# Layer 2 of a cross-attention kernel: scores of the first query half ahead of the values of two groups back

## The chip, the cores and the metric

One Trainium2 chip, of which one core is used. A core has five engines that run their own instruction streams and wait for each other through semaphores: TensorE (PE; its weight loads are shown as PEld), VectorE (DVE), ScalarE (ACT), GpSimd (POOL) and SyncE (SP, which here only issues transfers). Matmul results land in PSUM, which has eight banks of 128 x 512 floats; all else lies in SBUF. The metric is the device time of one execution in microseconds; three executions of the kernel before took 1634.38, 1636.12 and 1638.09 us, so the median is 1636.12 us.

## The reference

Two cross-attention layers, one after the other, on `x` of shape (16, 256, 320) with a context of (16, 256, 512): 16 batches, 256 queries, 320 channels in 20 heads of 16, 252 text tokens and 4 image tokens. Each layer does this (cut; `l2norm` only in the second):

```python
text, ip = ctx[:, :-4], ctx[:, -4:]
q, k, v = x @ Wq, text @ Wk, text @ Wv                # in heads of 16
text_out = softmax(q_h @ k_h.T * scale) @ v_h         # 256 x 252 scores per head
scores   = q_h @ k_ip_h.T * scale                     # 256 x 4 per head
# layer 1 adds to the image scores a term from softmax(q @ k.T) over all channels
# layer 2 adds a similarity to the image scores and
# normalises, with l2norm, what it attends to
out = (text_out + mask * softmax(fused) @ v_ip_h) @ Wout + bout + x
```

All of it is in fp32. The kernel keeps that precision by splitting operands into a rounded high part and a remainder, so a product of two fp32 matrices becomes several matmuls.

## The kernel before

The unit of work is a *slot*: one group of four heads of one batch. Layer 1 is slots 0 to 79 (`slot0`), layer 2 slots 80 to 159 (`slot1`, 16 batches x 5 groups); slots 160 and 161 finish. Slot functions are generators: they yield pieces of work, and between them a number, the place in the slot up to which a list of other tasks with due times is run (`fill`): projections of queries (L528), keys and values (L205), the end of a batch (`close1`), the opening of a later one, transfers of rows (`stacks`). These *fill tasks* differ from slot to slot and repeat every five slots.

In a slot of layer 2, for group k:

- `attend1(k - 2)`: P, the values of the group two slots back, 16 matmuls of 128 x 32 weights (L823) into one PSUM bank, then W, 16 more with the remainder `wt` against a constant (L826). `settle1` follows it: DVE transposes the bank into `nt` (L870), takes a reciprocal (L873) and multiplies into `hsn` (L874); POOL copies the norm parts (L871).
- `both1(k, 0)`: T, the transposed scores of group k for the first key half (4 matmuls, L775, two PSUM banks); S, the scores of group k + 2 for the first query half (4 matmuls, L780, a tile of two banks); DVE's reduction of S to row maxima `mn` (L781); and two exponentials on ACT from T into P (L786). `both1(k, 1)` is the same for the second half.
- `norm1(k - 1, u, n)`: products of the rounded weights `ctb` with `gm` (L814), in groups of 4 and 3 matmuls, four groups per slot, called (0,0), (0,1), (1,0), (1,1). DVE multiplies each group's bank into `wt` (L815), which also frees the bank.
- `rounded1`: ACT rounds P into `ctb` (L804), POOL writes the remainder to `wt` (L805).
- `maxima(k + 2)`: two matmuls (L792) turn the maxima, ACT copies them (L794) and issues two transfers into the query rows (L796). T of group k + 2 reads them as an extra row; it makes the exponential of a score less its maximum.

Only PE's order is fixed, by the order of the program; the order on DVE, ACT and POOL and the PSUM bank of each tile are chosen by a scheduler when the program is built (`schedule_with_timeline_sim=True, auto_bufs=True`). Tiles have tags: S (one tile of two banks), T (2), P (1) and X (3), the last for all else. P in SBUF has four buffers, two per slot: the exponentials of group k write the buffers that the values of group k - 2 read.

Two kinds of slots come up below. In the last part of one slot per batch `close1` does three small products (L931) whose results DVE adds to `hT` (L932). In the next slot ACT rounds `hT` (L517) and DVE makes the remainder `ho` (L518, L519), on which L528 runs later. Called here the slot before the split and the slot with the split.

Of the kernel before, what the change touches and what calls it, by code (L numbers as in the profile page):

```python
# [37 lines left out]
NS = B * NG  # L38
# [10 lines left out]
def xattn2(  # L49
# [39 lines left out]
    def bank(tag="X"):  # L89
        return ps.tile([128, 512], F32, tag=tag, name=tag, bufs=BANKS[tag])  # L90

    def scores():

        return ps.tile([128, 1024], F32, tag="S", name="S", bufs=1).rearrange("p (h t) -> p h t", h=4)
# [4 lines left out]
    def buf(tag, shape, dtype=F32, bufs=1, name=None):  # L99
        if tag in ("wB", "wD", "vr", "raw"):  # L100
            return sb.tile(shape, dtype, tag=tag, name=name or tag, bufs=bufs)
        size = 1
        for d in shape[1:]:
            size *= d
        if tag not in slots:
            slots[tag] = [0, dtype] + [const_tile([128, max(size, words.get(tag, 0))], f"{tag}_{i}", dtype) for i in range(bufs)]
        n, kind, *ring = slots[tag]
        assert kind == dtype and len(ring) == bufs, tag
        slots[tag][0] += 1
        t = ring[n % bufs][: shape[0], :size]  # L110
        names = "abcd"[: len(shape) - 1]
        if len(names) > 1:
            t = t.rearrange(f"p ({' '.join(names)}) -> p {' '.join(names)}", **dict(zip(names, shape[1:])))
        return t
# [26 lines left out]
    def anchor(inst):  # L141
        anchors[inst.ins.engine] = inst
        return inst
# [540 lines left out]
    def attend0(k):  # L684
        b, g = divmod(k, NG)
        v, pv = get("v0", b), bank("P")
        for vt in range(3):
            values0(k, pv, v, vt)
        settle0(b, g, pv)
# [68 lines left out]
        yield from project(l, wo[l], hh, evac)  # L758
        return y

    def both1(k, t):

        a = k + 2 < 2 * NS and QK[k + 2] 
        c = NS <= k < 2 * NS and QK[k]
        if a:
            if t == 0:
                maxes[k + 2] = buf("mn", [128, 4, 4], FR, bufs=2)[:, :2]
            sp = scores()
        if c:
            st = [bank("T").rearrange("p (h t) -> p h t", h=2) for u in range(2)]  # L770
            lo = (0, DUP)[t]
            for j in range(2):
                for u in range(2):
                    rows = slice(64 * u, 64 * u + KS1)
                    mm(st[u][:, j], c[1][rows, j, lo : lo + 128], c[0][rows, j], start=True, stop=True)  # L775
        if a:
            for j in range(2):
                for u in range(2):
                    rows = slice(64 * u, 64 * u + XROW)
                    mm(sp[:, 2 * u + j], a[0][rows, j, t * 128 : (t + 1) * 128], a[1][rows, j], start=True, stop=True)  # L780
            anchor(nc.vector.tensor_reduce(maxes[k + 2][:, t], sp[:, :, :T1], axis=AX.X, op=ALU.max))  # L781
        if c:
            for u in range(2):
                if t == 0:
                    P[k, u] = buf("P", [128, 2, 2, S], bufs=SIZES["NP"])
                anchor(nc.scalar.activation(P[k, u][:, t], st[u], AF.Exp, scale=SCALE))  # L786
# [13 lines left out]
    def rounded1(k, u):  # L800
        R[k, u] = buf("ctb", [128, 2, 2, S], FR, bufs=SIZES["CTB"], name="ph")
        W[k, u] = buf("wB", [128, 2, 2, S], bufs=SIZES["WB"], name="wt")
        for t in range(2):
            nc.scalar.activation(R[k, u][:, t], P[k, u][:, t], AF.Copy, scale=0.5)  # L804
            anchor(nc.gpsimd.tensor_sub(W[k, u][:, t], P[k, u][:, t], f(R[k, u][:, t])))  # L805
# [3 lines left out]
    def norm1(k, u, n):  # L809

        gm = get("t1", k // NG - B)[1]
        yp = bank().rearrange("p (h t) -> p h t", h=2)
        for i, (gb, kt) in enumerate(blocks[n]):
            mm(yp, gm[:, gb], R[k, u][:, kt], start=i == 0, stop=i == len(blocks[n]) - 1)  # L814
        nc.vector.tensor_mul(W[k, u][:, n], yp, W[k, u][:, n])  # L815

    def attend1(k):
        b, g = divmod(k - NS, NG)
        v, pv = get("t1", b)[0], bank("P")
        for n in range(2):  # L820
            for s in range(4):
                h = V1W * (4 * g + s)
                mm(pv[32 * s : 32 * s + 32, :S], v[:, n, h : h + 32], P[k, s % 2][:, n, s // 2], start=n == 0, stop=False)  # L823
        for n in range(2):
            for s in range(4):
                mm(pv[32 * s : 32 * s + 32, :S], zone, W[k, s % 2][:, n, s // 2], start=False, stop=n == 1)  # L826
        settle1(b, g, pv)

    def slot1(k):
        last = k - 1 if NS < k <= 2 * NS else None  # L830
        mine = k < 2 * NS
        if k == NS:
            yield lambda: maxima(k + 1)
        elif k == NS + 1:
            yield lambda: attend0(k - 2)
        else:
            yield lambda: attend1(k - 2)
        yield lambda: both1(k, 0)
        if last:
            yield lambda: norm1(last, 0, 0)  # L840
        yield 0.33
        if last:
            yield lambda: norm1(last, 0, 1)
        yield lambda: both1(k, 1)
        if mine:
            yield lambda: rounded1(k, 0)
        yield lambda: stacks(k + LEAD)
        if last:
            yield lambda: norm1(last, 1, 0)
        yield 0.67  # L850
        if last:
            yield lambda: norm1(last, 1, 1)
        if mine:
            yield lambda: rounded1(k, 1)
        yield lambda: maxima(k + 2)
        yield 1.0
# [3 lines left out]
    def settle1(b, g, pv):  # L860
        hn = hsn
        if g == 0:
            norms[b] = buf("tmp", [128, NG, 8, 6], bufs=2, name="n1")
        nt = norms[b]
        if "na" not in w1:
            w1["na"], masks = [buf("nt", [128, 2, 8, 32], bufs=2, name="na") for i in range(2)]
            w1["bmask"] = masks.rearrange("p a f c -> p (a f c)")[:, :CP]
            dma(w1["bmask"], bmask_d)
        na = w1["na"][:, (NG * b + g) % 2]
        nc.vector.transpose(na.rearrange("p f c -> p (f c)"), pv[:, :S])  # L870
        nc.gpsimd.tensor_copy(nt[:, g], na[:, :, 16:22])  # L871
        rz = pv[:, S : S + 8]
        nc.vector.reciprocal(rz, na[:, :, 16])  # L873
        nc.vector.tensor_mul(  # L874
            hn[:, g // 2, :, g % 2], na[:, :, 0:16], rz.unsqueeze(2).to_broadcast([128, 8, 16])
        )
        if g == NG - 1:
            nc.gpsimd.tensor_copy(hn[:, 2, :, 1], hn[:, 2, :, 0])
            later(0.4, lambda: gather(1, b))
# [98 lines left out]
    def get(*key):  # L978
        while key not in results:
            step(key)  # L980
        return results[key]
# [27 lines left out]
    for c in range(B // 2):  # L1009
        n, k = 10 * c, [("k0", c)] if c else []  # L1010
# [30 lines left out]
    def stacks(k):  # L1041
        if 0 <= k < 2 * NS:
            (stacks0 if k < NS else stacks1)(k)

    def ahead(k, t):
        if k < NS:
            score0(k, t)
        else:
            both1(k - 2, t)

    def maxima(k):
        if k < 2 * NS:
            (maxima0 if k < NS else maxima1)(k)
# [41 lines left out]
    with tc.manual_schedule(engines=PINNED):  # L1095
        for k in range(2 * NS + 2):
            clock[0] = k
            for part in (slot0 if k < NS else slot1)(k):
                if callable(part):
                    part()  # L1100
                else:
                    fill(k + part)
        fill(999)
# [81 lines left out]
```

## Time and profile before

| what | value |
|---|---|
| median of three executions | 1636.12 us |
| the profiled execution, its span | 1630.48 us, 1628.7 us |
| granted TensorE clock, mean over the span | 0.974 |
| layer 2, steady part (840 to 1550 us) | granted clock 1.00 |
| PE / DVE / POOL / ACT busy, whole span | 94% / 74% / 73% / 51% |
| matmuls of layer 2, 780 to 1600 us: L814, P, W, T, S | 316.4, 82.4, 81.4, 76.6, 62.0 us busy |
| DVE reduction L781, 128 x 1008 | 160 of 1195 ns |
| ACT exponential L786, 128 x 512 | 320 of 597 ns |
| period of a batch in the steady part (P at 1000.24 and at 1055.44) | 55.20 us |

A row of the timeline gives the start in microseconds, the busy time of the group, engine, line, operation, output and input, tile and count, and in brackets the idle time before it and who ended it. Matmul ends are modelled, and consecutive groups overlap in the table; the time from one start to the next says what a group costs PE.

### The profile page before, as it was taken

The numbers are of one execution on the slowest core, as the hardware profiler recorded it, in microseconds if no ns is written. First come the engines' busy times: TensorE is split into PE (matmuls) and PEld (weight loads), VectorE is DVE, ScalarE is ACT, GpSimd is POOL, SyncE is SP. The second block draws the span as 40 slices with busy tenths as digits, with TensorE's granted clock in tenths as the row PEclk, the third lists the DMA queues.
The fourth block names the chain that finished last, engine by engine and source line by source line (L and its number), as shares of the span: only waits on it lengthen the run. The fifth ranks groups of instructions, "written<-read, shape, count | busy, mean of one in ns | idle before, by whom it ended". The sixth has DMA issues, their size and how long they took to land.

```text
span 1628.7 us, 36230 instructions
## 1 busy us (share of the span) xinstructions
PE 1533.9 (94%) x13306; PEld 1232.8 (76%) x13306; DVE 1209.1 (74%) x2410; ACT 830.2 (51%) x1797; POOL 1189.4 (73%) x1147
## 2 busy tenths in 40 slices
PE   7899999999999898789999999999999999999996
PEld 6677878787878777577777777777777777777765
DVE  5567777777777668778877787778777877778685
ACT  5345455555555545445555555555554555555462
POOL 3358787878787767777678767866877687668676
PEclk9799999999999999899999999999999999999998
DMA  7767677767676666665514342433244334323301
GB/s 218 201 203 203 199 193 219 202 204 206 202 208 198 181 206 172 164 187 171 159 62 129 108 139 84 135 110 125 89 134 120 110 103 127 127 89 102 108 26 45
DMA packets 235741, 243.06 MB, mean 149 GB/s; under 512 B 19050, under 2 KB 219468, under 8 KB 235564
## 3 DMA queue, kind: packets, MB, share of 16 engines
q1 hardware_dynamic: 233356, 239.44, 49.4%
q8 instruction: 106, 1.74, 0.4%
q10 hardware_dynamic: 2208, 1.30, 0.3%
q14 instruction: 71, 0.58, 0.1%
HBM read 116.78 MB, written 88.18 MB: 126 GB/s over the span
## 4 chain that ended last, share of the span: by engine, by line
PE 52%; DVE 15%; POOL 11%; DMA 9%; ACT 6%; issue 4%; SPq 2%; ACTq 0%; POOLq 0%; DVEq 0%
PE X L205 15%; PE X L814 9%; PE X L528 7%; PE P L709 5%; POOL wt L805 4%; PE S L652 3%; POOL P L682 3%; PE P L823 3%; DMA qs<-qd 3%; PE P L826 2%; PE T L676 2%; PE T L775 2%; DVE wt L815 2%; DMA kd<-kst 2%; DVE mn L781 2%
## 5 line engine op out<-in xcount | busy, mean ns | idle before, releaser
L682 POOL TENSOR_TENSOR P<-P,rs 128x512 f32<-128x512 f32 x320 | 413.2, 1312 | 157.4 <-ACT P L679 157.0
L805 POOL TENSOR_TENSOR wt<-P,ctb 128x512 f32<-128x512 f32 x320 | 422.4, 1336 | 120.3 <-ACT ctb L804 118.7
L814 PE MATMUL X<-ctb,gm 128*128 128x512 f32 x1120 | 328.8, 411 | 2.5 <-DVE wt L815 2.5
L679 ACT ACTIVATE P<-T 128x512 f32<-128x512 f32 x320 | 175.9, 595 | 221.4 <-PE T L676 106.1
L786 ACT ACTIVATE P<-T 128x512 f32<-128x512 f32 x320 | 174.2, 597 | 144.1 <-PE T L775 123.3
L815 DVE TENSOR_TENSOR wt<-X,wt 128x512 f32<-128x512 f32 x320 | 216.7, 678 | 24.9 <-PE X L814 22.5
L804 ACT ACTIVATE ctb<-P 128x512 fp32r<-128x512 f32 x320 | 195.7, 631 | 73.1 <-PE X L814 57.9
L814 PEld LDWEIGHTS X<-ctb,gm 128*128 128x128 f32 x1120 | 188.8, 188 | 49.4 <-DVE wt L815 5.2
L781 DVE TENSOR_REDUCE mn<-S 128x4 fp32r<-128x1008 f32 x160 | 191.1, 1195 | 0.8 <-PE S L780 0.8
L654 DVE TENSOR_REDUCE mn<-S 128x4 fp32r<-128x716 f32 x160 | 142.6, 891 | 0.0
L676 PE MATMUL T<-qs,ks 127*128 127x256 f32 x640 | 112.1, 295 | 22.0 <-DMA qs<-mt 10.2
L709 PE MATMUL P<-P,vr 128*32 128x256 f32 x1920 | 129.4, 404 | 2.2 <-DVE mx L581 2.2
L652 PE MATMUL S<-ks,qs 125*128 125x256 f32 x640 | 117.4, 307 | 5.4 <-DVE mn L654 2.0
L652 PEld LDWEIGHTS S<-ks,qs 125*128 125x128 f32 x640 | 88.2, 194 | 41.8 <-issue 34.0
L894 POOL TENSOR_TENSOR r<-u,rs 128x40 f32<-128x40 f32 (+2 forms) x17 | 108.7, 6394 | 14.8 <-DVE u L891 14.7
L528 PE MATMUL X<-ho,wF 128*128 128x256 f32 x768 | 112.8, 290 | 6.4 <-DVE ho L518 3.0
L528 PE MATMUL X<-hq,wE 128*128 128x256 f32 x768 | 110.1, 287 | 7.5 <-ACT hq L517 3.2
L676 PEld LDWEIGHTS T<-qs,ks 127*128 127x128 f32 x640 | 92.8, 198 | 27.0 <-DVE tmp L726 11.6
L528 PEld LDWEIGHTS X<-ho,wF 128*128 128x128 f32 x768 | 103.5, 195 | 12.1 <-DVE ho L518 4.7
L528 PEld LDWEIGHTS X<-hq,wE 128*128 128x128 f32 x768 | 102.4, 193 | 12.0 <-ACT hq L517 3.6
L205 PE MATMUL X<-cta,wA 128*128 128x252 f32 (+1 forms) x720 | 100.6, 286 | 8.7 <-ACT wA L147 6.3
L205 PEld LDWEIGHTS X<-cta,wA 128*128 128x128 f32 x720 | 93.8, 194 | 15.2 <-ACT wA L147 6.5
(197 smaller groups left out, 2807.5 us busy)
## 6 DMA issues: line engine op xcount, KB each, us to landing
qd<-q SPq DMA_DIRECT2D x96, 384.0 KB
qs<-tph SPq DMA_DIRECT2D x64, 308.0 KB
kd<-kst SPq DMA_DIRECT2D x73, 256.0 KB
rawc<-in_cT_dram SPq DMA_DIRECT2D x60, 256.0 KB
qs<-qd SPq DMA_DIRECT2D x80, 192.0 KB
ks<-kd SPq DMA_DIRECT2D x80, 192.0 KB
ks<-kd SPq DMA_DIRECT2D x160, 96.0 KB
qs<-qd SPq DMA_DIRECT2D x160, 96.0 KB
```

Of the source, the lines that this page charges most:

```text
L205: last = mm(out, lhs(a, k), rhs(b, k), start=i == 0, stop=i == len(terms) - 1)
L528: mm(pp, w(s, k, slice(m * 128, (m + 1) * 128)), a[:, t], start=i == 0, stop=i == len(terms) - 1)
L652: mm(sp[:, h], Q[: XROW + T0, h, t * 128 : (t + 1) * 128], K[: XROW + T0, h], start=True, stop=True)
L676: mm(st[p][:, j], K[:KS0, 2 * p + j, t * 128 : (t + 1) * 128], Q[:KS0, 2 * p + j], start=True, stop=True)
L679: exp = anchor(nc.scalar.activation(pt, st[p], AF.Exp, scale=SCALE))
L682: anchor(nc.gpsimd.tensor_mul(pt, pt, rs[:, t : t + 1].to_broadcast([128, 2, S])))
L709: mm(pv[32 * s : 32 * s + 32, o : o + S], v[:, vt, h : h + 32], P[k, s // 2][:, t, s % 2], start=vt < 2, stop=vt != 1,)
L781: anchor(nc.vector.tensor_reduce(maxes[k + 2][:, t], sp[:, :, :T1], axis=AX.X, op=ALU.max))
L804: nc.scalar.activation(R[k, u][:, t], P[k, u][:, t], AF.Copy, scale=0.5)
L805: anchor(nc.gpsimd.tensor_sub(W[k, u][:, t], P[k, u][:, t], f(R[k, u][:, t])))
L814: mm(yp, gm[:, gb], R[k, u][:, kt], start=i == 0, stop=i == len(blocks[n]) - 1)
L815: nc.vector.tensor_mul(W[k, u][:, n], yp, W[k, u][:, n])
```

## The change

The values of two groups back no longer open the slot. They are handed to `both1(k, 0)` as a function, which calls it after the reduction of S and before the exponentials. In slots 82 to 159 PE's order at the slot's opening was P, W, T, S and is now T, S, P, W; `settle1` moves with P and W. In slots 160 and 161, which have no scores, the order stays. Nothing is added or taken away. DVE's, ACT's and POOL's orders and the banks are chosen anew by the scheduler.

```diff
-    def both1(k, t):
+    def both1(k, t, between=None):
 
         a = k + 2 < 2 * NS and QK[k + 2] 
         c = NS <= k < 2 * NS and QK[k]
...
             anchor(nc.vector.tensor_reduce(maxes[k + 2][:, t], sp[:, :, :T1], axis=AX.X, op=ALU.max))
+        if between:
+            between()
         if c:
             for u in range(2):
                 if t == 0:
...
             yield lambda: maxima(k + 1)
         elif k == NS + 1:
             yield lambda: attend0(k - 2)
-        else:
-            yield lambda: attend1(k - 2)
-        yield lambda: both1(k, 0)
+        yield lambda: both1(k, 0, (lambda: attend1(k - 2)) if k > NS + 1 else None)
         if last:
             yield lambda: norm1(last, 0, 0)
         yield 0.33
```

As built, DVE has the reduction of the first S ahead of L870, L873 and L874 in nearly all slots of layer 2; in the slot with the split it stands directly behind L519. ACT issues the L796 transfers behind the exponentials in one slot per batch. SP's order is the same. The banks of layer 2 were shared among all tags; now S has two of its own, T two, P one, and X goes round three.

## The prediction

> **What bounds the kernel now.** I read the page's head and its busy table first, then the table by windows, then the waits of PE, and last the rows of PE and DVE over one batch of layer 2. The whole program:
>
> ```profile
> span 1628.7 us, 36230 instructions
> PE 1533.9 (94%) x13306; PEld 1232.8 (76%) x13306; DVE 1209.1 (74%) x2410; ACT 830.2 (51%) x1797; POOL 1189.4 (73%) x1147
> 1000.00:1050.00 50.00, 49.21 (x440) 38.02 (x439) 37.45 (x71) 26.65 (x56) 37.18 (x37) 1.00 0.34 106
> ```
>
> PE is busy for 94% of the span. The third line is a window of layer 2, the only layer that the change touches: PE 49.21 of 50 us at a granted clock of 1.00, DVE 37.45, ACT 26.65, POOL 37.18. No other engine is near to its end there, so only two things can move the time: PE's own cost of another order, and the little that PE waits. The waits of PE between 780 and 1600 us:
>
> ```profile
> PE S L780 <- DVE mn L781: 7.1, 14, 1.1
> PE X L814 <- DVE wt L815: 2.5, 13, 0.2
> ```
>
> Scores wait for the reduction that empties S, and the norm products wait for a bank, once per batch. These are idle times after modelled ends. Counted from start to start they are larger, as the rows of one batch show (first two slots of five):
>
> ```profile
> 998.04 1.46 PE L931 MATMUL X<-rs,rs 128*128 128x256 f32 x6
> 999.21 0.99 PE L814 MATMUL X<-ctb,gm 128*128 128x512 f32 x3
> 1000.24 1.07 PE L823 MATMUL P<-P,v1t 128*32 128x256 f32 x16
> 1001.13 1.05 PE L826 MATMUL P<-wt,zone 128*32 128x256 f32 x16
> 1002.11 0.50 PE L775 MATMUL T<-qs,ks 50*128 50x256 f32 x4
> 1002.45 0.40 PE L780 MATMUL S<-ks,qs 48*128 48x256 f32 x4
> 1002.78 1.19 PE L814 MATMUL X<-ctb,gm 128*128 128x512 f32 x4
> ...
> 1005.98 0.50 PE L775 MATMUL T<-qs,ks 50*128 50x256 f32 x4
> 1006.97 0.50 PE L780 MATMUL S<-ks,qs 48*128 48x256 f32 x4 [0.49 <-DVE mn L781]
> 1007.66 1.19 PE L814 MATMUL X<-ctb,gm 128*128 128x512 f32 x4 [0.19 <-DVE wt L815]
> ```
>
> Undisturbed, T to S takes 1002.45 - 1002.11 = 0.34 and S to L814 0.33. In the second half of this slot they take 0.99 and 0.69, so 0.65 + 0.36 = 1.01 us are lost. The cause is DVE in the same slot:
>
> ```profile
> 994.77 0.45 DVE L921 STREAM_TRANSPOSE rs<-rs 128x256 f32<-128x256 f32 x1 [1.23 <-POOL rs L914]
> 995.31 1.19 DVE L781 TENSOR_REDUCE mn<-S 128x4 fp32r<-128x1008 f32 x1
> ...
> 1001.64 1.59 DVE L518 TENSOR_TENSOR ho<-hT,ho 128x512 fp32r<-128x512 f32 x1 [0.30 <-ACT ho L517]
> 1003.15 1.51 DVE L519 SCALAR_TENSOR_TENSOR ho<-ho,tmask,hT 128x256 fp32r<-128x256 f32 x1
> ...
> 1005.75 1.16 DVE L781 TENSOR_REDUCE mn<-S 128x4 fp32r<-128x1008 f32 x1
> ```
>
> S was full at 1002.85, but its reduction started at 1005.75, behind the split of ho (3.1 us) and L922, L739 and the L870 transpose. This is the slot with a spell of long DVE work; the three other slots of the batch lose nothing at S. The slot before loses about 0.24 (0.11 at S, 0.13 at L792). Fourteen whole batches of 55.2 us lie in the steady part.
>
> **The change, part by part.** In slots 82 to 159 PE issued P (L823), W (L826), T, S; it now issues T, S, P, W. Slots 160 and 161 hold neither scores nor exponentials and keep their order. No matmul, reduction, copy or transfer is added; SP's queue is unchanged in the built program.
>
> *PE's own cost.* From the rows: P to W 0.89, W to T 0.98, T to S 0.34, S to L814 0.33, together 2.54. Behind the same predecessor, T starts after the same time as P (L792: 0.21 in both cases; L205 with wA: 1.57 in both). W is left in 0.98 for L814 too (the one such place, 1597.17 to 1598.15). So the new order costs 0.34 + (S to P) + 0.89 + 0.98, and only S to P is not in the trace. The nearest row is S to L814, 0.33: with it the sum is 2.54 again, and the cost nothing. Bounds: products to P start 0.13 earlier than products to products (L528: 0.95 against 1.09), and T to S and S to X differ by under 0.1, so at best 0.24, -0.09 per slot; at worst P and its 32-column weights cannot be set up beside S, and the 0.18 by which other entries differ is added, +0.19. Over the 76 slots that have both S and P: -6.8 to +14.4 us. I take 0 by the nearest row.
>
> The Trainium skill speaks against the change here: "TensorEngine Tiling (Array Packing)", Tiling Modes, Key Properties, says that changing the tiling mode drains TensorE, and S (row tiles) to P (column tiles) is such a change. Priced as S's busy 0.40 less the 0.33 after which its successor starts, a drain would give 0.07 x 76 = +5 us. The row speaks for less: S to L814 is a change of mode as well and takes 0.33, and both orders hold three changes per first half.
>
> *The slot before the split of ho (990.84 to 1000.24).* S starts at 990.84 + 0.34 = 991.18 instead of 993.05. Its reduction fits into the 1.23 us in which DVE waits for POOL's L914 (993.3 to 994.8), where nothing covers it now. Then L921 994.77, L870, L873, L874, and wt00 (L815) starts at 996.08 instead of 996.43; everything behind it is 0.35 earlier, wt10 ends at 999.39 instead of 999.74. But in the built program the X tiles of layer 2 go strictly round three banks, where before they also used others. The third product of L931 must have the bank of the L814 group three tiles back, which wt10 frees: it starts at 999.45, where the run of matmuls alone gives 998.66. From there L814 0.33, L792 0.70, next slot 0.21: 1000.69 against 1000.24. So +0.45: the wait at S goes, and a larger one at L931 comes.
>
> *The slot with the split.* T 1000.69, S 1001.03, P 1001.36, W 1002.25, L814 1003.23, and by the durations of the rows T 1006.43, S 1006.77 with no wait, as the reduction now stands directly behind L519. L517 starts 0.19 later (its three L932 follow the late L931), so L518 1001.83, L519 1003.34, reduction 1004.78, L922, L739, L870, then wt00 from 1007.05 to 1007.72. The second L814 group waits for that bank: 1007.78, against 1007.66 now. Thus the 1.01 at S and L814 has gone, but the time was DVE's, whose chain L517 to wt00 is as long as before. The batch ends +0.12, x 14 = +1.7 us.
>
> *The bank ring elsewhere.* In the other slots the reuse comes 0.06 to 0.8 us after the release, by the present rows; cost nothing, but the cover is thin. *ACT:* exps now wait for P of two groups back, whose buffers they overwrite; they start some 0.6 us earlier than now all the same. In one slot per batch the two transfers of the maxima (L796) are issued behind them, about 2 us later; T needs them more than 9 us after the issue. L804 and L147 queue behind the exps as before. *DVE:* settle (L870, L873, L874) comes after the reduction; hsn is read again at L739 more than 5 us later. *POOL:* L871 moves behind one L148 (1.29 us) in one slot per batch; only the image softmax 5 slots on reads it.
>
> *Ends of the layer.* At 782.82 W waits for wt11 (W takes 1.72 to T, not 0.98); it now comes 0.67 later in the slot: -0.7. At 1555.33 T to S takes 1.55 through the same wait as above, in a slot with no L931 in it: -1.2.
>
> Sum: 0 + 1.7 - 0.7 - 1.2 = -0.2 us. The profiled execution took 1630.48 us (span 1628.7), 5.6 less than the median of 1636.12; the difference carries over to the median: 1635.9. A change under 0.2% (3.3 us) cannot be told from none for this kernel.
>
> Apart from the sum: the Trainium skill, "SBUF — State Buffer", Who interferes with whom, says that a DVE instruction with two SBUF inputs and a GpSimd instruction that reads SBUF contend for a port pair, and that the later one blocks fully. L518 at 1.59 us beside POOL's L805, and 0.69 at 1603.95 without it, agree. By that rule L519 ends with POOL's instruction however late it began, and the batch would come out at -0.08 instead of +0.12, -2.8 us in all.
>
> **The rivals.**
> A, *DVE's relief is real* (faster). The third product of L931 does not wait, or waits half. For it: 1.24 us of waits per batch stand at exactly these places, and DVE is idle 1.23 us where the reduction would now go. Against it: wt10 frees the bank. If all goes: -1.24 x 14 - 1.9 = -19 us (1617); with half of it about -9 (1627).
> B, *S to P costs* (slower). Its place is each of 76 slots; from 0.043 us per slot it decides (3.3 / 76). At 0.1, +7.6 (1643.5); at 0.19, +14.4 (1650). Against it: leaving S costs 0.33 wherever else it is left.
> C, *the ring of three banks bites oftener* (slower). The margins of 0.06 to 0.8 us fall short in more slots, or the whole ho chain is shifted by the 0.45 too: +0.4 per batch, +5.6 (1641.5); up to +0.9, 1648.5.
> That the reduction does not move is excluded: in the built DVE order it stands before the transpose.
>
> **How the numbers follow.** Forecast (within about 3 us of 1635.9) 0.40; A 0.29; B 0.14; C 0.17. The forecast alone spans 1632 to 1639.5. The range reaches to three quarters of A and to two thirds of B and C: 1620 to 1645. Faster: A and 0.06 of the forecast, 0.35. Slower: B, C and 0.03 of it, less 0.01 of C that stays inside, 0.33. Same: 0.32.
>
> **What would show it.** In the changed profile: S to P of 0.33; no wait of S for mn in the second halves; waits of about 0.8 at L931 or the L814 behind it, released by DVE wt; L814 after the second S 0.7 after it in the split slot; the batch still 55.2 us long. A batch of 54 us speaks for A; one of 55.7 with S to P near 0.43 for B; one of 55.6 with new waits at L814, L205 or L792 for C. A late T behind L796 would prove the ACT reading wrong.

## The result, and the profile after

In comparisons of fifteen runs each, the changed kernel took 1628.12 us (1624.5 to 1633.45) and the kernel before 1633.88 us (1628.77 to 1638.09). The ratio is 0.9971 with a 95% interval of 0.9961 to 0.9981: 0.29% faster, 3.1 to 6.4 us, about 4.7. The forecast was no change that can be measured (1635.9 us, -0.2 us), the range 1620 to 1645. The time lies in the range, but the interval of the ratio excludes 1: there is a gain, a small one.

The profiled execution of the changed kernel is the longer of the two, 1631.7 against 1628.7 us:

```profile
span 1631.7 us, 36363 instructions
PE 1540.0 (94%) x13306; PEld 1235.5 (76%) x13306; DVE 1215.7 (75%) x2410; ACT 828.8 (51%) x1797; POOL 1188.4 (73%) x1147
```

That is not the change. The first T of layer 2 starts at 750.8 us in this trace and at 744.3 in that of the kernel before, after instructions that are the same in both programs; in the traces of this study it started anywhere from 741.0 to 750.9. So spans are of no use here, and everything below is counted from the opening of slot 82 on. From there to the start of the last group of matmuls the two traces of the kernel before took 858.6 and 858.8 us, those of the changed kernel 855.0 and 854.5: 3.9 us less, within the interval above.

Where that lies, from the same openings (the first P or T of a slot to that of the next):

| stretch | before | after | difference |
|---|---|---|---|
| slots 82 to 96 | 164.4, 164.6 | 162.4, 162.1 | -2.2 |
| slots 97 to 151 (11 batches) | 607.0, 607.0 | 606.1, 606.0 | -1.0 |
| slots 152 to 158 | 58.1, 58.0 | 57.5, 57.5 | -0.5 |
| slot 159 to the end | 29.2, 29.2 | 29.0, 29.0 | -0.2 |

In a batch of the steady part three slots are unchanged to 0.03 us. The slot before the split went from 9.41 to 10.08 us, the slot with the split from 13.01 to 12.27, the batch from 55.18 to 55.09.

The waits of PE from 780 to 1600 us in the changed kernel (columns: who waits for whom, us in all, times, the longest; L817 is the old L815, L816 the old L814, L825 and L828 the old L823 and L826, L794 on PE the old L792; two single waits of 0.9 and 0.4 are left out):

```profile
PE X L931 <- DVE wt L817: 6.5, 12, 0.6
PE X L816 <- DVE wt L817: 1.1, 5, 0.5
```

The wait of S for its reduction, 7.1 us in 14 places before, has gone from the list. In its place stands the wait of the products L931 for the release of a bank by wt, 6.5 us in 12 places. PE's rows of one slot before the split and of the split slot that follows it:

```profile
1001.24 1.19 PE L816 MATMUL X<-ctb,gm 128*128 128x512 f32 x4
1002.28 1.02 PE L931 MATMUL X<-rs,rs 128*128 128x256 f32 x4
1003.87 0.70 PE L931 MATMUL X<-rs,rs 128*128 128x256 f32 x2 [0.57 <-DVE wt L817]
1004.22 1.04 PE L816 MATMUL X<-ctb,gm 128*128 128x512 f32 x3
1005.10 0.28 PE L794 MATMUL X<-ident_r,mn 128*4 128x128 f32 x2
1005.31 0.50 PE L775 MATMUL T<-qs,ks 50*128 50x256 f32 x4
1005.65 0.40 PE L780 MATMUL S<-ks,qs 48*128 48x256 f32 x4
1005.98 1.07 PE L825 MATMUL P<-P,v1t 128*32 128x256 f32 x16
1006.86 1.05 PE L828 MATMUL P<-wt,zone 128*32 128x256 f32 x16
1007.84 1.20 PE L816 MATMUL X<-ctb,gm 128*128 128x512 f32 x4
...
1011.04 0.50 PE L775 MATMUL T<-qs,ks 50*128 50x256 f32 x4
1011.38 0.40 PE L780 MATMUL S<-ks,qs 48*128 48x256 f32 x4
1011.94 1.19 PE L816 MATMUL X<-ctb,gm 128*128 128x512 f32 x4 [0.15 <-DVE wt L817]
```

S to P is 1005.98 - 1005.65 = 0.33, as S to L814 was; over all 76 slots the median is 0.329. T to S, P to W and W to L816 take 0.34, 0.88 and 0.98 here, as in the other order. The new order costs PE nothing. T to S in the second half is 0.34, undisturbed, and the L816 behind it loses 0.56 - 0.33 = 0.23 instead of 0.36. The third of the three products of L931 (two matmuls each) starts 1.59 after the first; in the kernel before, all six matmuls took 1.17 until the next group started. DVE's rows of the same two slots:

```profile
996.67 1.19 DVE L781 TENSOR_REDUCE mn<-S 128x4 fp32r<-128x1008 f32 x1
999.23 0.45 DVE L921 STREAM_TRANSPOSE rs<-rs 128x256 f32<-128x256 f32 x1 [1.37 <-POOL rs L914]
...
1003.13 0.68 DVE L817 TENSOR_TENSOR wt<-X,wt 128x512 f32<-128x512 f32 x1
...
1006.28 1.33 DVE L518 TENSOR_TENSOR ho<-hT,ho 128x512 fp32r<-128x512 f32 x1 [0.29 <-ACT ho L517]
1007.54 1.50 DVE L519 SCALAR_TENSOR_TENSOR ho<-ho,tmask,hT 128x256 fp32r<-128x256 f32 x1
1008.96 1.20 DVE L781 TENSOR_REDUCE mn<-S 128x4 fp32r<-128x1008 f32 x1
1010.08 0.54 DVE L922 TENSOR_TENSOR rs<-rs,nt 128x384 f32<-128x384 f32 x1
```

The reduction of the first half is done early, but then DVE stands still for 1.37 us at L921, with the settling and every later `wt` behind it. wt10 (the third row shown) ends at 1003.81; the waiting product starts at 1003.87. In the split slot the reduction stands where L922 stood. POOL's rounding remainders there (L807 is the old L805):

```profile
1005.78 2.97 POOL L807 TENSOR_TENSOR wt<-P,ctb 128x512 f32<-128x512 f32 x2
```

### The profile page after: what moved, and what is told of

The parts are those of the page before. It is cut to its first block, busy times and chain, and to the rows that moved or that the text cites. A ratio compares the mean times of both kernels' runs of the same rounds, so it can differ in the third digit from the quotient of the medians.

```text
span 1631.7 us, 36363 instructions
## 1 busy us (share of the span) xinstructions
PE 1540.0 (94%) x13306; PEld 1235.5 (76%) x13306; DVE 1215.7 (75%) x2410; ACT 828.8 (51%) x1797; POOL 1188.4 (73%) x1147
## 4 chain that ended last, share of the span: by engine, by line
PE 55%; DVE 13%; DMA 10%; POOL 9%; ACT 4%; issue 3%; SPq 3%; ACTq 0%; POOLq 0%; DVEq 0%
PE X L205 15%; PE X L816 12%; PE X L528 7%; PE P L709 5%; PE P L825 3%; DMA qs<-mt 3%; POOL P L682 3%; PE S L652 3%; PE P L828 3%; DMA qs<-qd 3%; PE T L775 3%; SPq L82 2%; PE T L676 2%; DVE wt L817 2%; DVE ho L518 2%
## 5 line engine op out<-in xcount | busy, mean ns | idle before, releaser
L807 POOL TENSOR_TENSOR wt<-P,ctb 128x512 f32<-128x512 f32 x320 | 422.3, 1335 | 93.0 <-ACT ctb L806 91.3
L816 PE MATMUL X<-ctb,gm 128*128 128x512 f32 x1120 | 330.4, 413 | 2.1 <-DVE wt L817 1.1
L816 PEld LDWEIGHTS X<-ctb,gm 128*128 128x128 f32 x1120 | 189.2, 188 | 72.3 <-issue 15.6
L817 DVE TENSOR_TENSOR wt<-X,wt 128x512 f32<-128x512 f32 x320 | 218.2, 683 | 33.9 <-PE X L816 28.4
L528 PE MATMUL X<-ho,wF 128*128 128x256 f32 x768 | 112.8, 290 | 6.3 <-DVE ho L518 3.0
L528 PE MATMUL X<-hq,wE 128*128 128x256 f32 x768 | 111.5, 289 | 7.1 <-ACT hq L517 3.3
L528 PEld LDWEIGHTS X<-ho,wF 128*128 128x128 f32 x768 | 103.2, 194 | 12.6 <-DVE ho L518 4.7
L528 PEld LDWEIGHTS X<-hq,wE 128*128 128x128 f32 x768 | 103.5, 195 | 11.7 <-ACT hq L517 3.7
L205 PE MATMUL X<-cta,wA 128*128 128x252 f32 (+1 forms) x720 | 100.9, 286 | 7.3 <-ACT wA L147 5.7
L205 PEld LDWEIGHTS X<-cta,wA 128*128 128x128 f32 x720 | 94.1, 195 | 12.5 <-ACT wA L147 5.9
```

Of the source, the lines that this page charges most:

```text
L205: last = mm(out, lhs(a, k), rhs(b, k), start=i == 0, stop=i == len(terms) - 1)
L528: mm(pp, w(s, k, slice(m * 128, (m + 1) * 128)), a[:, t], start=i == 0, stop=i == len(terms) - 1)
```

## Experiments

All ratios are to the kernel before on the same chip. The lengths are means over the 11 batches of slots 97 to 151, worked out from the openings of the slots in each trace. PSUM banks are numbered as in the built programs; the traces do not show them.

| kernel | slot before the split | split slot | batch | ratio (95%) |
|---|---|---|---|---|
| before | 9.41 | 13.01 | 55.18 | |
| null_before | 9.41 | 13.01 | 55.18 | 1.0009 (0.9995 to 1.0022) |
| again_after | 10.07 | 12.28 | 55.09 | 0.9972 (0.9959 to 0.9986) |
| split_slots_only | 9.41 | 12.59 | 54.77 | 0.9947 (0.9932 to 0.9962) |
| turn_late | 9.48 | 12.03 | 54.25 | 0.9908 (0.9892 to 0.9923) |
| prods_slots_only | 9.23 | 13.04 | 55.04 | 0.9986 (0.9971 to 1.0002) |
| third_in_p | 9.64 | 12.03 | 54.74 | 0.9943 (0.9921 to 0.9965) |
| before_turn_late | 9.23 | 13.04 | 55.04 | 0.9987 (0.9973 to 1.0002) |
| split_turn | 9.29 | 11.70 | 53.75 | 0.9877 (0.9851 to 0.9903) |
| before_no922 | 9.23 | 12.02 | 54.01 | 0.9894 (0.9876 to 0.9913) |
| before_only922 | 9.41 | 12.87 | 55.05 | 0.9978 (0.9962 to 0.9994) |
| split_no922 | 9.23 | 11.70 | 53.69 | 0.9854 (0.9835 to 0.9873) |

### Both kernels once more

The kernel before, unchanged. 

> The kernel before, unchanged, against itself, to see what the comparison makes of nothing and to have a second profile of it. Both theories: ratio 1.000 within 0.001. Slot lengths in the profile as in the first one, to 0.03 us (slot before the split 9.41, slot with the split 13.01, batch 55.18); the time up to the first T of layer 2 may differ by some us between executions, since 744 and 750.5 us were seen for the same instructions.

The changed kernel, unchanged. 

> The changed kernel, unchanged. In the two profiles layer 2 (first to last T) became shorter by about 1.6 us only, while the timed ratio of 0.9971 stands for 4.7 us. Theory 1 (layer 2 is the whole of it, and the first profile was a poor sample): ratio 0.997 again, and in this profile T of slot 81 to the last T comes out near 827 us. Theory 2 (layer 2 gives 1.6 us and the rest is scatter of the executions): ratio nearer to 0.999, and layer 2 again 830 us, with 10.09 us for the slot before the split and 12.27 for the split.

The null came out at 1.0009, its interval holds 1. The changed kernel gave 0.9972 again. Both theories on the record missed a point. The slots were as theory 2 had them, 10.07 and 12.28. But the 1.6 us from which both set out was a counting error: it was taken from T to T, and before the change T lies 1.87 us behind the opening of its slot, while now it is the opening. Counted from opening to opening, layer 2 accounts for 3.9 of the 4.7 us, and nothing needs to be looked for outside it.

### Which of the two slots makes the gain

The new order in the split slots alone:

```diff
-        yield lambda: both1(k, 0, (lambda: attend1(k - 2)) if k > NS + 1 else None)
+        late = k > NS + 1 and (k - NS) % 5 == 4
+        if k > NS + 1 and not late:
+            yield lambda: attend1(k - 2)
+        yield lambda: both1(k, 0, (lambda: attend1(k - 2)) if late else None)
```

> The new order only in the slot with the split (slots 84, 89, ...), the old one in all others. Theory A (the chain of DVE from L517 to wt00 sets when the second L814 group may start, whatever PE's order): with the reduction directly behind L519, S no longer waits but L814 does; wt00 ends at 1007.53 instead of 1007.60 of the rows before, so 0.0 to 0.1 us per batch, ratio 0.999 to 1.000. Theory B (the split slot's own gain of 0.74 us is the change's doing there, and the 0.68 lost in the slot before is a separate cost that this kernel avoids): -0.74 x 14 = -10 us, ratio 0.994.

And in the slots before the split alone, the same with `== 3`:

> The new order only in the slot before the split (slots 83, 88, ...), the old one in all others, the split slot among them. Theory A (what the changed kernel loses in the slot before and gains in the split slot is one and the same delay: the chain of DVE from the last L932 to wt00 keeps its time, and PE arrives at it later): the slot before becomes 10.05 to 10.1 us, the split slot gets shorter by as much although its own order is the old one, 12.0 to 12.35 us, with the wait of S for its reduction gone; the batch 54.8 to 55.2 us, ratio 0.996 to 1.000. Theory B (the new order in the split slot makes its gain): the split slot stays at 13.0, the batch is 55.85, ratio 1.006.

The first gave 0.9947, better than the whole change: the split slot lost 0.42 us and the slot before kept its 9.41. The ratio is near theory B's, but not the 0.74 that the slot was to lose, and the cause is for the most part neither theory's. The L814 behind the second S starts 7.30 us after the slot's opening instead of 7.41 (means of the 11 batches), which is what theory A allows, and it still waits for wt00:

```profile
1002.06 1.21 PE L816 MATMUL X<-ctb,gm 128*128 128x512 f32 x4 [0.61 <-DVE wt L817]
```

The other 0.3 lie at the end of the slot. There L205 starts 0.12 behind the maxima (L792) instead of 0.38: it no longer waits for L537, since as built it has another bank than the product that L537 reads, where before they shared one.

The second gave 0.9986. The slot before the split got shorter, 9.23 instead of the 10.05 both theories expected, where the third product was built with bank 5 and not, as in the changed kernel, with the one that wt10 frees (2); no wait at L931 is left. The split slot stayed at 13.04, so theory A fell: S waits as ever, although DVE came to L519 1.83 instead of 2.91 us after the slot's opening (before_turn_late below shows why). The two slots are separate matters.

### The wait at L931

In the changed kernel, L921 is queued behind the settling of its slot:

```diff
-        nc.vector.tensor_mul(
+        results["settled"] = nc.vector.tensor_mul(
             hn[:, g // 2, :, g % 2], na[:, :, 0:16], rz.unsqueeze(2).to_broadcast([128, 8, 16])
         )
...
-        nc.vector.transpose(pT, pi.rearrange("p f c -> p (f c)"))
+        queued(nc.vector.transpose(pT, pi.rearrange("p f c -> p (f c)")), results["settled"])
```

> The changed kernel with one DVE instruction moved: L921, the transposition that DVE holds at its head for 1.37 us while POOL's L914 runs, now comes behind the settling (L870, L873, L874) of the slot before the split. PE, ACT, POOL, SP and the banks are the same. Theory A (the wait of the third product at L931 is the late wt10, late because DVE stood still at L921): wt10 ends some 0.6 us earlier, the wait at L931 falls from 0.57 to under 0.15, the slot before the split from 10.09 to about 9.45, the split slot stays near 12.3; -0.65 x 14 = -9 us on top of the change, ratio to the kernel before 0.991 to 0.993. Rival (the wait is replaced by the next, at L814 for the bank of the first product, or the split slot gives the time back as its DVE chain keeps its pace): ratio 0.996 to 0.998, as the change alone.

0.9908, at the edge of theory A's 0.991 to 0.993; the split slot, which theory A left near 12.3, fell to 12.03. DVE's rows of the slot before the split, then PE's:

```profile
988.20 0.45 DVE L870 STREAM_TRANSPOSE nt<-P 128x256 f32<-128x256 f32 x1 [0.20 <-PE P L828]
988.68 0.21 DVE L873 RECIPROCAL P<-nt 128x8 f32<-128x8 f32 x1
988.93 0.29 DVE L874 TENSOR_TENSOR hsn<-nt,P 128x128 f32<-128x128 f32 x1
989.58 0.45 DVE L921 STREAM_TRANSPOSE rs<-rs 128x256 f32<-128x256 f32 x1 [0.36 <-POOL rs L914]
...
992.80 0.69 DVE L817 TENSOR_TENSOR wt<-X,wt 128x512 f32<-128x512 f32 x1
```

```profile
992.60 1.65 PE L931 MATMUL X<-rs,rs 128*128 128x256 f32 x6
993.89 1.04 PE L816 MATMUL X<-ctb,gm 128*128 128x512 f32 x3
```

The settling now fills the time in which DVE stood still, 0.36 of 1.37 us is left, wt10 starts 7.27 us after the slot's opening (985.53) instead of 7.87, and the six products run through. PE's order and the orders of ACT, POOL and SP are those of the changed kernel, and so are the banks but for a few outside these slots. The slot falls from 10.08 to 9.48. So 0.6 of the 0.68 us that the change loses in this slot are shown to come from DVE standing at L921.

The same wait attacked from its other end: the third product gets a bank of another tag.

```diff
-                ip = bank()[:, :S]
+                ip = bank("P" if p == 2 else "X")[:, :S]
```

> The changed kernel with the third product of L931 in a bank of the tag P, which is free there, instead of the X ring. Theory (ring): the wait of 0.57 at L931 goes, and the next in the ring, L814 (1,1), waits for the same wt10 until about 0.35 us before its present start; the slot before the split falls from 10.08 to about 9.55 and the split slot stays within 0.2 of 12.27, though the scheduler now has the reduction ahead of L518 there; -0.5 x 14 = -7 us on top of the change, ratio 0.992 to 0.994. Rival (the wait is for DVE's work whatever the bank: L932 or the split come as late as before): the slot before gets shorter, the split slot longer by as much, ratio 0.997.

0.9943. The wait at L931 disappeared and the slot before the split took 9.64 (expected 9.55), so the late wt10 acts through the bank. The split slot fell to 12.03, just outside the 0.2 allowed, with DVE's order there changed by the scheduler. The slot behind it grew from 10.43 to 10.75, because the last L205 there starts 0.38 behind the maxima instead of 0.12, the size of the wait at L205 named above. As built it shares a bank there with the product that L537 reads, and in the changed kernel it does not; no run gave it another bank alone.

### Is PE's new order needed at all?

The kernel before with its PE order, and L921 behind L874 and the first reduction, which takes DVE's standstill away (`results["settled"]` as above):

```diff
-        nc.vector.transpose(pT, pi.rearrange("p f c -> p (f c)"))
+        queued(nc.vector.transpose(pT, pi.rearrange("p f c -> p (f c)")), results["settled"], anchors[mybir.EngineType.DVE])
```

> The kernel before, its PE order untouched, with L921 put behind L874 and the reduction of the first S on DVE, so that DVE does not stand 1.23 us at L921. Theory A (all waits of the kernel before come from DVE's late chain, and that from the stand at L921): the chain of the split slot comes 0.9 us earlier, S waits no more, L814 under 0.15; the slot before 9.41 to 9.2, the split slot 13.01 to about 12.2, the batch 54.2, ratio 0.991 to 0.992, which is as much as the changed kernel with the same move. Rival (PE's order matters: with the old one the reduction in the split slot stays behind L739 and L870, and S waits all the same): the split slot above 12.7, ratio 0.995 or more.

0.9987, an interval that holds 1: the rival, and a surprise. DVE, POOL and PE in the split slot:

```profile
1001.46 0.95 DVE L518 TENSOR_TENSOR ho<-hT,ho 128x512 fp32r<-128x512 f32 x1 [0.29 <-ACT ho L517]
1002.33 1.51 DVE L519 SCALAR_TENSOR_TENSOR ho<-ho,tmask,hT 128x256 fp32r<-128x256 f32 x1
1003.76 1.64 DVE L922 TENSOR_TENSOR rs<-rs,nt 128x384 f32<-128x384 f32 x1
...
1006.01 1.16 DVE L781 TENSOR_REDUCE mn<-S 128x4 fp32r<-128x1008 f32 x1
```

```profile
1000.56 1.30 POOL L148 TENSOR_TENSOR cta<-rawc,cta 128x512 fp32r<-128x512 f32 x1
1001.81 3.17 POOL L805 TENSOR_TENSOR wt<-P,ctb 128x512 f32<-128x512 f32 x2
```

```profile
1007.23 0.50 PE L780 MATMUL S<-ks,qs 48*128 48x256 f32 x4 [0.51 <-DVE mn L781]
```

POOL in the same slot of the first profile:

```profile
1001.40 2.98 POOL L805 TENSOR_TENSOR wt<-P,ctb 128x512 f32<-128x512 f32 x2
```

Against the first profile, DVE came to L519 at 1.85 instead of 2.91 us after the slot's opening (1000.48 here, 1000.24 there). It came to L739 at 4.84 instead of 4.81. All of the lead was lost in L922, which took 1.64 us instead of 0.55 and ended at 1005.40, 0.42 behind POOL's second L805 (1001.81 + 3.17 = 1004.98). The reduction behind it did not move.

The same move with the new order in the split slots:

> The new order in the split slots only, with L921 behind L874 and the reduction in the slot before. Theory A: both gains add, the slot before 9.2, the split slot 11.8 to 12.0 (L814 there waits under 0.15, no wait at L205), the batch 53.95 to 54.1, ratio 0.987 to 0.990, ahead of the changed kernel with the move alone (0.9908). Rival (one wait is behind both, so the gains do not add): the batch 54.25 or more, ratio 0.991 to 0.993.

0.9877: more than the two gains taken together (0.53% and 0.13%). Here the reduction is in L922's place, beside POOL's second L807, and the lead is kept:

```profile
993.67 0.95 DVE L518 TENSOR_TENSOR ho<-hT,ho 128x512 fp32r<-128x512 f32 x1 [0.29 <-ACT ho L517]
994.54 1.50 DVE L519 SCALAR_TENSOR_TENSOR ho<-ho,tmask,hT 128x256 fp32r<-128x256 f32 x1
995.97 1.19 DVE L781 TENSOR_REDUCE mn<-S 128x4 fp32r<-128x1008 f32 x1
997.08 0.54 DVE L925 TENSOR_TENSOR rs<-rs,nt 128x384 f32<-128x384 f32 x1
```

```profile
994.03 3.17 POOL L807 TENSOR_TENSOR wt<-P,ctb 128x512 f32<-128x512 f32 x2
```

The reduction takes its 1.19 us while POOL works, and L925 (the old L922) its 0.54 as POOL ends at 997.20. Is it then the new order of PE, or only that L922 is not next to POOL? L922 can be moved without PE: it makes an operand for the L931 of the next batch. `held`, taken where `image_softmax` begins, is the last reduction of S given to DVE until then:

```diff
+        held = anchors[mybir.EngineType.DVE]
...
-        nc.vector.tensor_mul(vb, vb, w1["bmask"])
+        queued(nc.vector.tensor_mul(vb, vb, w1["bmask"]), held)
```

With L921 late, and PE's old order:

> The kernel before with L921 late as in before_turn_late, and L922 taken out of the split slot: it is queued three slots earlier in the batch. PE's order is that of the kernel before. Seen before this run: with L921 late, DVE reached L922 0.8 us earlier, but L922 then lasted 1.64 us instead of 0.55, until POOL's two L805 were done, and nothing was gained. Theory P (DVE instructions with two SBUF inputs stand still beside POOL's; the new order gains in the split slot only because the reduction, which reads PSUM, takes L922's place there): without L922 the reduction ends at about 1006.25 on the clock of before_turn_late, S does not wait, the split slot falls from 13.04 to 12.0 to 12.2, the batch to 54.0 to 54.25, ratio 0.990 to 0.992, with the old PE order. Rival (PE's new order is needed for the gain): the split slot stays above 12.7, ratio 0.996 or more.

Alone, in the kernel before:

> The kernel before with L922 alone moved out of the split slot. Theory P: L518 and L519 stay pinned to POOL's L805 (L519 ends at about 1004.65 on the clock of the first profile), L739, L870, L873, L874 follow, the reduction starts 0.2 us earlier at most and wt00 ends 0.3 earlier; the split slot 12.7 to 12.85, ratio 0.996 to 0.998. Rival (L922 is the only thing in the way): the split slot falls by the whole 1.0 us that PE waits, to 12.0, ratio 0.991.

As it ran, L922 came not three slots earlier but two slots later than before, 8.0 us into the second slot behind the split and still ahead of its L931; there it took its usual 0.55. The first gave 0.9894, just beyond theory P's 0.990 to 0.992, with the split slot (12.02) and the batch (54.01) as theory P had them. DVE and PE in the split slot:

```profile
998.42 1.51 DVE L519 SCALAR_TENSOR_TENSOR ho<-ho,tmask,hT 128x256 fp32r<-128x256 f32 x1
999.86 0.43 DVE L739 STREAM_TRANSPOSE hT<-hsn 128x256 f32<-128x256 f32 x1
...
1001.10 1.20 DVE L781 TENSOR_REDUCE mn<-S 128x4 fp32r<-128x1008 f32 x1
```

```profile
1002.31 0.50 PE L775 MATMUL T<-qs,ks 50*128 50x256 f32 x4
1002.65 0.40 PE L780 MATMUL S<-ks,qs 48*128 48x256 f32 x4
1002.99 1.19 PE L814 MATMUL X<-ctb,gm 128*128 128x512 f32 x4
```

L739, L870, L873 and L874 run beside POOL, whose two L805 last from 997.90 to 1001.08, at their usual length, and PE waits neither at S nor at L814, in the order of the kernel before. The scheduler also dealt the banks anew and put L873 and L874 ahead of the reduction. Up to the last L814 of the split slot, PE starts everything behind the second S at the same place as in split_turn (6.41 and 9.36 us after the opening in both). What is left of the difference, 12.02 against 11.70, lies behind it, in the wait of L205 for the bank that L537 frees:

```profile
1006.53 0.42 DVE L537 TENSOR_TENSOR q<-X,q 128x256 fp32r<-128x256 f32 x1 [0.60 <-ACT q L536]
1006.63 0.28 PE L792 MATMUL X<-ident_r,mn 128*4 128x128 f32 x2
1007.01 1.65 PE L205 MATMUL X<-cta,wA 128*128 128x252 f32 x12
```

In split_turn L205 has another bank and starts 0.12 behind the maxima. So in the split slot PE's new order is not needed. Two moves on DVE gain 1.06%, more than three times the change. L922 alone gave 0.9978: the split slot at 12.87, 0.14 less than before and just outside theory P's 12.7 to 12.85. Here L518 (1.57 us) and L519 (1.52) stayed beside POOL, and L873 and L874 again stand ahead of the reduction. So neither move on DVE is enough without the other.

Last, everything that helped together (the new order in the split slots, L921 late, L922 moved):

> The new order in the split slots only, L921 late, and L922 out of the split slot. In split_turn the batch took 53.75 us and PE waited 0.2 us in it, so there is little left. Theory P: ratio 0.986 to 0.988, the batch 53.6 to 53.75. Rival (L922 collides with POOL where it stands now and delays something there): 0.989 or more.

0.9854, 1609.4 us: the shortest time of the study and slightly ahead of the expectation, but not clear of split_turn (the intervals overlap, and the batch takes 53.69 against 53.75).

## Why the prediction was right or wrong

The places were right, and so was the mechanism in the slot before the split; in the split slot a step of it was wrong, and with it the sum: -0.2 us forecast, 3.9 us counted in the traces and 4.7 timed. That the time lies in the range is owed to the range, which reaches 15.9 us below the forecast. Of the 7.8 us between 1635.9 and 1628.12 another 2.2 are no miss of the reasoning: the three executions from which the forecast started gave 1636.12, the fifteen of the comparison 1633.88. Step by step:

- *PE's own cost, 0.* Right: S to P 0.329 in the median of 76. Rival B is gone. The drain that the Trainium skill, "TensorEngine Tiling (Array Packing)", Tiling Modes, Key Properties, states, priced at 0.07, is not seen in these rows: S to P takes no longer than T to S (0.34), which changes no mode (both use tiles of 64 rows), and by its modelled end S still ran when P started. One reading behind the bounds was the wrong way round: in the rows of before L528 to P takes 1.09 and L528 to products 0.95, so products to P start later, not earlier. No term of the sum rests on it.
- *The slot before the split, +0.45.* Right in its cause, shown by turn_late, third_in_p and prods_slots_only: bank, wt10, L921. Short by 0.2, nearly all of it between L816 and L794 (0.88 where 0.70 was taken). The kernel before already took 0.82 in this place (999.21 to 1000.03), of which the prediction had called 0.13 a wait; turn_late, where L931 waits for nothing, took 0.88 too. "Strictly round three banks" was too strong; some tiles of the other slots go to a fourth or fifth.
- *The split slot, -0.33.* It was -0.74. The step that failed is "the chain L517 to wt00 is as long as before". It lasted 6.83 us before (1000.77 to 1007.60), 6.76 in the prediction's own numbers (1000.96 to 1007.72) and 6.46 after (1005.43 to 1011.89). I took L518's 1.59 us as its duration, but it holds a wait for POOL, and L518 started later against POOL's L805: 1.33. In both profiles it ended 1.83 behind the start of the first of POOL's two L805 (1001.40 and 1005.78). That is 0.26 of the 0.30. The rest of the miss is the 0.2 of the slot before: PE comes to the split slot that much later, the chain does not. The sentence set apart from the sum, by the port rule of the Trainium skill, "SBUF — State Buffer", Who interferes with whom, gave -0.08 per batch where the rows taken as durations gave +0.12. Measured: -0.09. I should have summed by it.
- *Per batch +0.12.* It was -0.09: over the 11 batches of slots 97 to 151 -1.0 us where the sum has +1.3, so 2.3 us of the miss of 3.7.
- *Start of the layer, -0.7.* With two batches at +0.12 the sum has -0.5 for slots 82 to 96, which gave -2.2. The wait for wt11 in slot 84 went as forecast (-0.66). Not counted were slot 82 (-0.43 and more; the wait of L205 at 764.7 for v1t), slot 85 (-0.3, L205 behind L792 again) and slots 88 to 90, where the first split after the start gave 0.44 net, with a loss of 0.24 only in the slot before. The first two stood in the trace of before as single waits, and I had left them standing without a reason.
- *End, -1.2.* With one batch at +0.12 the sum has -1.1, and it was -0.5 and -0.2: slot 154, where the wait of 1.21 at 1555 stood, gained 0.58 only, and slot 155 lost 0.35, of which 0.32 lies between T and S at its opening. Why is not shown.

Of the rivals, A (the relief is real) expected that L931 would not wait; it did, for the whole of the predicted time. The kernel ended between the forecast and A because both gains and losses were larger than taken, the gains by more.

## What to carry to other kernels

A duration read beside another busy engine may hold a wait. Before such a row goes into a sum for a new order, find the same instruction where the other engine is idle, and check what the instruction that takes its place reads. An instruction that waits at the head of an engine's order holds up everything behind it, as L921 did on DVE for 1.37 us. On top of the change, moving it behind work that was ready gained 0.6%, where the change itself had gained 0.3%; in the kernel before, the same move gained nothing that is clear of noise until L922 was moved as well. And where a scheduler deals out banks, compare the banks too; here two of the waits that came or went were banks dealt differently.

## What the runs showed of the hardware

I had not expected that DVE and POOL would hold each other up by whole instructions. Where POOL is idle, at the end of the kernel before, the three DVE instructions take 0.69, 0.48 and 0.56 us:

```profile
1603.95 0.69 DVE L518 TENSOR_TENSOR ho<-hT,ho 128x512 fp32r<-128x512 f32 x1
1604.56 0.48 DVE L519 SCALAR_TENSOR_TENSOR ho<-ho,tmask,hT 128x256 fp32r<-128x256 f32 x1
1605.06 0.56 DVE L922 TENSOR_TENSOR rs<-rs,nt 128x384 f32<-128x384 f32 x1
```

Beside POOL's L805 they took 0.70 to 1.77 (in third_in_p), 1.50 to 1.52 and up to 1.64 us. In the two rows where it can be read best, the end lies 0.3 to 0.4 us behind the end of POOL's instruction (L519 in the first profile 1004.66 against 1004.38, L922 in before_turn_late 1005.40 against 1004.98). POOL is held up too: two L805 in a row took 2.86 to 3.18 us instead of twice 1.29. All of these instructions have two inputs in SBUF. The reduction (1.19 to 1.20) and the multiplication `wt` (0.62 to 0.69), which read PSUM, and the transposition L739 (0.43), which has one input, kept their length. That agrees with what the Trainium skill, "SBUF — State Buffer", Who interferes with whom, states: a DVE instruction with two SBUF inputs contends with a GpSimd instruction that reads SBUF, one with at most one SBUF input and outside the 2-port modes does not. The runs add that which of two DVE instructions stands beside a busy POOL is enough to gain or lose a microsecond per batch: the L814 behind the second S starts 7.43 us after the opening in before_turn_late, with L922 there, and 6.41 in split_turn, with the reduction there, and in before_no922, with L739.
